# An RNN step beside an LSTM step: the RNN's product in exact bf16 parts, states of both in rings, histories copied by GpSimd

## The chip, the cores and the metric

The kernel runs on one core of one Trainium2 chip. A core has a matrix engine (TensorE, PE in the profile, its weight loads PEld), three engines for elementwise work (VectorE or DVE, ScalarE or ACT, GpSimd or POOL), a queue engine for transfers (SyncE or SP), an on-chip memory of 128 partitions (SBUF) and a smaller one that only TensorE's products land in (PSUM). The engines run side by side, each in the order of its own queue, and wait for one another through semaphores. The metric is the device time of one execution in microseconds (us); less is better.

## The reference

The program is four residual layers over x (4 sequences, 1024 steps, width 512), with a condition of 4 x 512 as the first state of both recurrences. The two recurrences matter here:

```python
xW = jnp.einsum('ntd,dh->nth', x, Wx) + b          # layer 0, RNN
def step(prev_h, xw_t):
    next_h = jnp.tanh(xw_t + prev_h @ Wh)          # 4 x 512 times 512 x 512
    return (next_h, next_h)
...
def step(carry, xw_t):                             # layer 2, LSTM
    prev_h, prev_c = carry
    A = xw_t + prev_h @ Wh                         # 4 x 512 times 512 x 2048
    i, f, o = (jax.nn.sigmoid(A[:, n * H:(n + 1) * H]) for n in range(3))
    g = jnp.tanh(A[:, 3 * H:])
    next_c = f * prev_c + i * g
    next_h = o * jnp.tanh(next_c)
    return ((next_h, next_c), next_h)
...
x = x + layer0(x); x = x + layer1(x); x = x + layer2(x); x = x + layer3(x)
```

Layer 1 is a small state-space model (SSM) with a 4-tap convolution in front; layer 3 multiplies every step by a matrix of its own for each sequence. All in fp32.

## The kernel before

All layers run in one stream. The 1024 steps lie in 32 chunks of 32 (TC). One pass of `do_pass` (L815) goes through the 32 LSTM steps of chunk c; the RNN is LEAD = 56 steps ahead of the LSTM, so the loop at L846 issues LSTM step s and RNN step s + 56 together, and around them the jobs of the layers between, each placed by hand at a step and a slot ("pe", "gap" or "end"; `do`, L841). The first 56 RNN steps run alone (the lead), the last 56 LSTM steps have no RNN. Every engine works in the order in which the loop issues its instructions; there is no planner.

The LSTM's product (`lstm_mm`, L375): h and the weights are each cut into three bf16 parts whose sum is the fp32 value exactly (`upper`, L202, takes the upper half of an fp32 word as bf16; `split`, L206, subtracts it to get the next part). The stationary operand is 12 columns, three parts of four sequences; the moving operand is one of three weight parts, 256 columns. Four products run at once in four column strips of the array. The accumulators of halves A and B (`acc2`) are turned by VectorE (L403), the three parts and the input summed by a reduction over the innermost axis (L409), gates and tanh done by ScalarE (L416, L439), products, cell and h by VectorE (L429, L434, L442), and the new h is split twice (L208). Half A's h is ready before half B's; the next step's products that need only A's half of h come first, and products of half B's gates last.

The RNN's product (`rnn_mm`, L349) is in fp32: 4 chunks of the width, 4 strips each, 4 stationary columns against 128. VectorE turns `acc0` (L368) and adds the projected input (L369); ScalarE's tanh (L372) writes the state into the history `h0`, from which the next step and the SSM read. In TensorE's queue it stands behind the LSTM's products and the step's job; in VectorE's, transpose and add stand behind the splits of half B and in front of half A's transpose of the next step.

The histories: `h0` (RNN) and `h2` (LSTM, with all three parts of each state) hold two chunks each. The SSM adds h0 to x (L461) and layer 3 adds h2 (L747). GpSimd has work only at the start.

Of the kernel before, what the change touches and what calls it, by code (L numbers as in the profile page):

```python
# [29 lines left out]
W2_BUFS = 4  # L30
NP = 3
EPS = 1e-5
XBUFS = 3


# [4 lines left out]
def cond_resid_kernel(ctx: ExitStack, tc: tile.TileContext, a: dict, out: bass.AP):  # L40
# [47 lines left out]
    def load_rows(pool, name, src, n, eng):  # L88

        t = pool.tile([P, KC, n], F32, name=name, tag=name)  # L90
        quads(eng, t, src.rearrange("(j c q) n -> j q c n", j=4, c=KC))
        return t
# [11 lines left out]
    x2 = [state.tile([P, KC, TC, B], F32, name=f"x2{i}", tag=f"x2{i}") for i in range(2)]  # L104
    xw2 = [state.tile([P, 4, KC, TC, B], F32, name=f"xw2{i}", tag=f"xw2{i}") for i in range(2)]

    h2 = [state.tile([P, KC, TC, NP, B], F32, name=f"h2{i}", tag=f"h2{i}") for i in range(2)]


    def turns(n, name, shape):  # L110
        return [state.tile(shape, F32, name=f"{name}{i}", tag=f"{name}{i}") for i in range(n)]

    tt2 = [turns(2, f"tt2{m}", [P, 4, 2, B + CT]) for m in range(2)]
    gc = [turns(4, f"gc{m}", [P, 5, 2, B]) for m in range(2)]
    prod = [turns(2, f"prod{m}", [P, 2, 2, B]) for m in range(2)]
    th2 = [turns(4, f"th2{m}", [P, 2, B]) for m in range(2)]
    tt0 = turns(1, "tt0", [P, KC, CT])
    pre0 = turns(2, "pre0", [P, KC, B])

    x1 = state.tile([P, KC, 3 + TC, B], F32, name="x1", tag="x1")  # L120
# [10 lines left out]
    quads(nc.scalar, condT, a["condT"].rearrange("(c q) j b -> j q c b", c=KC))  # L131
    load_x(0, a["xT"][0])
    wx0 = load_rows(const, "wx0", a["Wx0"], D, nc.sync)
    wh0 = load_rows(const, "wh0", a["Wh0"], D, nc.sync)

    prep_ctx = ExitStack()
    prep = prep_ctx.enter_context(tc.tile_pool(name="prep", bufs=1))
# [64 lines left out]
    def upper(x):  # L202

        return x.bitcast(BF16)[..., 1::2]

    def split(h, n):  # L206

        nc.vector.tensor_tensor(h[:, :, n], h[:, :, n - 1], upper(h[:, :, n - 1]), ALU.subtract)  # L208
# [4 lines left out]
    for h in h0:  # L213
        nc.vector.memset(h[:, :, TC - 1, :], 0.0)
    nc.vector.tensor_copy(h0[1][:, :, TC - 1, :], condT)
    nc.vector.tensor_scalar(h2[1][:, :, TC - 1, 0, :], condT, 2.0, None, ALU.mult)
    for n in range(1, NP):
        split(h2[1][:, :, TC - 1], n)
    for m in range(2):
        nc.vector.memset(gc[m][0][:, 3], 0.0)  # L220
    nc.vector.memset(x1[:, :, 0:3, :], 0.0)
# [67 lines left out]
    def split_wh2(k, g):  # L289

        w, scale, cols = layer[:, k, g], 1.0 if g == 3 else 0.5, slice(PLACE[g] * D, (PLACE[g] + 1) * D)
        part = [x[:, k, cols] for x in wh2]
        left = xw2[g % 2][:, 2 + g // 2].rearrange("p c t b -> p (c t b)")
        return (
            lambda: nc.scalar.activation(part[0], upper(w), AF.Copy, scale=scale),
            lambda: nc.vector.scalar_tensor_tensor(left, w, scale, part[0], ALU.mult, ALU.subtract),
            lambda: nc.scalar.copy(part[1], upper(left)),
            lambda: nc.vector.tensor_tensor(part[2], left, part[1], ALU.subtract),
        )
# [47 lines left out]


    def rnn_mm(c, t):  # L349
        h = h0[c % 2] if t else h0[(c - 1) % 2]  # L350
        for k in range(KC):
            for j in range(4):
                nc.tensor.matmul(  # L353
                    acc0[CT * j : CT * j + B, :],
                    h[:, k, (t - 1) % TC, :], wh0[:, k, j * P : (j + 1) * P],
                    start=(k == 0), stop=(k == KC - 1),
                )

    idle = bank("idle", [P, D], tag="ada", bufs=1)
# [1 line left out]
    def keep_busy():  # L361

        x = xin[0].rearrange("p c t b -> p (c t b)")
        tiled(idle, lambda j: x[:, :CT], x)

    def rnn_pre(c, t):
        tt, pre = tt0[0], pre0[t % 2]
        nc.vector.transpose(tt.rearrange("p c b -> p (c b)"), acc0)  # L368
        nc.vector.tensor_add(pre, xw0[c % 2][:, :, t, :], tt[:, :, :B])  # L369

    def rnn_h(c, t):
        nc.scalar.activation(h0[c % 2][:, :, t, :], pre0[t % 2], AF.Tanh)  # L372


    def lstm_mm(c, t, kh, mh, parts=range(2 * NP)):  # L375


        h = h2[c % 2] if t else h2[(c - 1) % 2]
        for x in parts:
            k, n = 2 * kh + x // NP, x % NP  # L380
            w = wh2[n][:, k].rearrange("p (g n) -> p g n", g=4)
            for j in range(4):
                n0 = P * j + 2 * CT * mh
                nc.tensor.matmul(  # L384
                    acc2[mh][CT * j : CT * j + NP * B, :],
                    upper(h[:, k, (t - 1) % TC].rearrange("p s b -> p (s b)")), w[:, :, n0 : n0 + 2 * CT],
                    start=(k == 0 and n == 0), stop=(k == KC - 1 and n == NP - 1),
                )

# [3 lines left out]
    class Half:  # L393


        def __init__(self, c, t, m):
            self.m, self.tt, self.gc, self.th = m, tt2[m][t % 2], gc[m][t % 4], th2[m][t % 4]
            self.prod, self.c = prod[m][t % 2], gc[m][(t + 1) % 4][:, 3]
            self.out = h2[c % 2][:, 2 * m : 2 * m + 2, t]


        def transpose(self, g0=0, g1=3):
# [42 lines left out]

        def split(self, n):
            split(self.out, n)

# [108 lines left out]
        nc.gpsimd.memset(r, 0.0)  # L559

    ae, xc, sq = (prep.tile([P, KC, B], F32, name=x, tag=x) for x in ("ae", "xc", "sq"))
    ones = xw2[0][:, 0, 0].rearrange("p t b -> p (t b)")
    nc.gpsimd.memset(ones, 1.0 / D)

    def mean_over_width(x):
# [115 lines left out]
    def at_step(i, f):  # L681

        c, t = divmod(i - LEAD, TC)
        at(c, t, f)
# [25 lines left out]
    for i in range(4 * KC + 3):  # L710
        for n, f in ((i - 3, 3), (i - 1, 1), (i - 2, 2), (i, 0)):
            if 0 <= n < 4 * KC:
                at_step(6 + i, stages[n][f])

    at_step(17, load_w1)
    for j in range(W2_BUFS):
        at_step((31, 33)[j // 2], lambda j=j: load_w2(j))
# [27 lines left out]

    def adapt_add(c, m, x3, t0=0, t1=TC):
        nc.vector.scalar_tensor_tensor(  # L747
            x3[:, m, :, t0:t1].rearrange("p b t -> p t b"), h2[c % 2][:, m, t0:t1, 0], 0.5, x2[c % 2][:, m, t0:t1],
            ALU.mult, ALU.add,
        )  # L750

# [63 lines left out]
    def do_pass(c, first=0, src=None, dst=None, last=None):  # L815

        lstm = c >= 0
        jobs = []
        if dst is not None:
            jobs += adapt_jobs(c - 1, dst)  # L820
        if c == NCHUNK - 1:
            more, rest = last_adapt(c, last)
            jobs += more
        if -1 <= c < NCHUNK - 1:
            jobs += ssm_jobs(c + 1)
            jobs += input_jobs(
                c + 1, 0, range(25, 29), ((28, "end"), (29, "gap"), (29, "end"), (30, "gap"))
            )
        if src is not None:
            jobs.append((9, "end", lambda: load_x(c + 4, src)))  # L830
        if c + 3 < NCHUNK:
            for m in range(KC):
                mm, end = project0(c + 3, m)
                t = (18, 20, 22, 30)[m]
                jobs += [(t, "pe", mm), (t, "end", end)]
        if lstm:
            jobs += input_jobs(c, 1, range(4), ((3, "end"), (4, "gap"), (4, "end"), (5, "gap")))
            jobs += input_jobs(c, 2, range(4, 8), ((8, "gap"), (8, "end"), (9, "gap"), (9, "end")))
            jobs += input_jobs(c, 3, range(9, 17, 2), ((15, "end"), (16, "gap"), (18, "gap"), (19, "gap")))

        def do(t, place):  # L841
            for slot, where, f in jobs:
                if (slot, where) == (t, place):
                    f()

        for t in range(first, TC):  # L846
            r = divmod(c * TC + t + LEAD, TC)
            rnn = r[0] < NCHUNK
            if lstm:
                A, Bh = Half(c, t, 0), Half(c, t, 1)  # L850
                lstm_mm(c, t, 0, 0)
                lstm_mm(c, t, 0, 1, (0, 1))
                lstm_mm(c, t, 1, 0)
                lstm_mm(c, t, 0, 1, (2, 3, 4, 5))
                lstm_mm(c, t, 1, 1)
            do(t, "pe")
            if rnn:
                rnn_mm(*r)
            if c * TC + t < 8 - TC:
                keep_busy()  # L860
            if lstm:
                A.transpose()
                A.sum()
                A.transpose_o()
                A.sum_o()
                A.gates()
                A.products()
                A.gate_o()
                Bh.transpose()
                A.cell()  # L870
                Bh.transpose_o()
                A.tanh()
                Bh.sum()
                Bh.gates()
                A.h()
                Bh.sum_o()
                A.split(1)
                Bh.gate_o()
                Bh.products()
                A.split(2)  # L880
                Bh.cell()
            do(t, "gap")
            if lstm:
                if (c, t) != (NCHUNK - 1, TC - 1):
                    for m in range(2):
                        lstm_input(c if t + 1 < TC else c + 1, (t + 1) % TC, m)
                Bh.tanh()
                Bh.h()
                Bh.split(1)
                Bh.split(2)  # L890
            if rnn:
                rnn_pre(*r)
                rnn_h(*r)
            do(t, "end")
            while later:
                later.pop()()
            for f in early.pop((c, t), ()):
                f()
        if last is not None:
            rest()  # L900
# [78 lines left out]
```

## Time and profile before

| | us |
|---|---|
| time, median of three runs | 4678.84 (4676.4 to 4680.62) |
| span of the profiled execution | 4689.2 |
| LSTM product L384, TensorE | 2908.8 busy, 98304 products |
| RNN product L353, TensorE | 1089.4 busy, 32768 records |
| transposes of the LSTM L403, VectorE | 1236.6 busy, 4096 |
| sums L409, VectorE | 1038.9 busy, 4096 |
| splits L208, VectorE | 673.2 busy, 4098 |
| RNN transpose L368 and add L369, VectorE | 316.3 and 180.2 busy, 1024 each |
| GpSimd, all | 48.7 busy, 91 instructions |

"Busy" of a group is the time in which at least one of its instructions was under way. TensorE's instructions overlap: a product is listed from its start until its result is in PSUM (273 ns for the LSTM's), while the next ones start long before. Consecutive VectorE instructions overlap too, when the later one does not need the earlier one's result.

### The profile page before, as it was taken

The page shows a single profiled execution, that of the slowest core. Times are in us where ns is not written, and L with a number is a line of the kernel's source. Part 1 is how long each engine was busy: PE and PEld are TensorE (multiplying, and loading weights), DVE is VectorE, ACT ScalarE, POOL GpSimd, SP SyncE. Part 2 cuts the span into 40 slices and gives each one's busy share as a digit, 9 for nine tenths or more (in the row PEclk, how much of TensorE's full clock was granted, in tenths as well). Part 3 has the DMA queues.
Part 4 walks back from the last instruction along what each step waited for, and adds up shares of the span by engine and source line. Part 5 has one row for each costly group of instructions (what it writes and reads, how often), then busy time and mean ns, then how long its engine had stood idle before and what let it go on. Part 6 is the DMA issues. An engine that isn't in the chain of part 4 may idle for free.

```text
span 4689.2 us, 326423 instructions
## 1 busy us (share of the span) xinstructions
PE 4552.4 (97%) x146816; PEld 3581.8 (76%) x146816; DVE 3956.1 (84%) x22102; ACT 1876.6 (40%) x9693; POOL 48.7 (1%) x91
## 2 busy tenths in 40 slices
PE   7999999999999999999999999999999999999986
PEld 5777777777877777777777877777777777777754
DVE  4688888888888888888888888888888888888876
ACT  3334444444444444443444444444443444444333
POOL 3000000000000000000000000000000000000000
PEclk9999999999999999999999999999999999999999
DMA  6300000000000000000000000000000000000000
GB/s 155 102 24 7 9 7 9 9 7 9 9 7 9 9 7 9 9 7 9 9 7 9 9 7 9 9 7 9 9 7 9 9 7 9 9 5 7 6 6 8
DMA packets 40234, 67.77 MB, mean 14 GB/s; under 512 B 8864, under 2 KB 26016, under 8 KB 38320
## 3 DMA queue, kind: packets, MB, share of 16 engines
q1 hardware_dynamic: 35792, 46.55, 3.7%
q8 instruction: 1147, 18.79, 1.7%
q14 instruction: 255, 2.09, 0.1%
q0 software_dynamic: 1696, 0.19, 0.0%
q10 hardware_dynamic: 1344, 0.14, 0.0%
HBM read 38.34 MB, written 8.39 MB: 10 GB/s over the span
## 4 chain that ended last, share of the span: by engine, by line
PE 91%; DVE 7%; issue 1%; DMA 0%; POOL 0%; ACT 0%; SPq 0%; DVEq 0%; POOLq 0%
PE acc L384 55%; PE acc L353 18%; PE proj L334 9%; PE pb L308 3%; DVE tt L403 3%; DVE gc L409 2%; PE proj L308 2%; PE ada L754 2%; DVE prod L429 1%; PE ssm_out L308 1%; DVE h L208 1%; PE idle L308 0%; PE pp L616 0%; DVE h L442 0%; DVE tt L368 0%
## 5 line engine op out<-in xcount | busy, mean ns | idle before, releaser
L384 PE MATMUL acc<-wh,h 128*12 128x256 bf16 x98304 | 2908.8, 273 | 96.6 <-DVE h L208 91.0
L384 PEld LDWEIGHTS <-h 128*12 128x12 bf16 x98304 | 2316.3, 87 | 549.0 <-DVE h L208 194.0
L403 DVE STREAM_TRANSPOSE tt<-acc 128x192 f32<-128x192 f32 (+1 forms) x4096 | 1236.6, 310 | 291.0 <-PE acc L384 267.8
L416 ACT ACTIVATE gc<-gc 128x24 f32<-128x24 f32 (+1 forms) x4096 | 854.4, 216 | 1388.5 <-DVE gc L409 1382.9
L353 PEld LDWEIGHTS acc<-wh,h 128*4 128x4 f32 x32768 | 811.6, 87 | 498.9 <-issue 204.2
L353 PE MATMUL acc<-wh,h 128*4 128x128 f32 x32768 | 1089.4, 273 | 12.4 <-ACT h L372 6.6
L409 DVE TENSOR_REDUCE gc<-tt 128x24 f32<-128x96 f32 (+1 forms) x4096 | 1038.9, 255 | 70.5
L208 DVE TENSOR_TENSOR h<-h 128x8 f32<-128x8 f32 (+1 forms) x4098 | 673.2, 164 | 69.9
L372 ACT ACTIVATE h<-pre 128x16 f32<-128x16 f32 x1024 | 221.6, 216 | 1130.9 <-DVE pre L369 1130.9
L439 ACT ACTIVATE th<-gc 128x8 f32<-128x8 f32 x2048 | 427.9, 209 | 261.9 <-DVE gc L434 225.4
L334 PE MATMUL proj<-wx,x 128*32 128x512 f32 x4096 | 530.5, 592 | 0.3 <-issue 0.3
L442 DVE SCALAR_TENSOR_TENSOR h<-gc,th 128x8 f32<-128x8 f32 x2048 | 328.8, 161 | 143.6 <-ACT th L439 133.9
L368 DVE STREAM_TRANSPOSE tt<-acc 128x128 f32<-128x128 f32 x1024 | 316.3, 309 | 68.9 <-PE acc L353 68.8
L429 DVE SCALAR_TENSOR_TENSOR prod<-gc 128x16 f32<-128x16 f32 x2048 | 348.7, 170 | 12.7
L391 ACT COPY tt<-xw 128x32 f32<-128x32 f32 x2048 | 327.9, 207 | 0.0
L434 DVE SCALAR_TENSOR_TENSOR gc<-prod 128x8 f32<-128x8 f32 x2048 | 298.6, 146 | 0.0
L369 DVE TENSOR_TENSOR pre<-xw,tt 128x16 f32<-128x16 f32 x1024 | 180.2, 176 | 37.6
L308 PE MATMUL proj<-xin,wx 128*32 128x128 f32 x4096 | 138.6, 277 | 17.5 <-DMA wh<-in_Wh_dram 11.8
L754 PE MATMUL ada<-layer,x 128*32 128x512 f32 (+1 forms) x1056 | 134.8, 587 | 2.7 <-DVE x L747 2.6
L308 PE MATMUL pb<-x,wp 128*32 128x128 f32 x4096 | 134.7, 273 | 1.0 <-issue 0.6
L308 PEld LDWEIGHTS proj<-xin,wx 128*32 128x32 f32 x4096 | 117.0, 112 | 22.1 <-DMA wh<-in_Wh_dram 11.8
L334 PEld LDWEIGHTS proj<-wx,x 128*32 128x32 f32 x4096 | 119.6, 110 | 5.5 <-issue 0.5
(125 smaller groups left out, 1159.1 us busy)
## 6 DMA issues: line engine op xcount, KB each, us to landing
layer<-in_w2T_dram SPq DMA_DIRECT2D x32, 512.0 KB, 4.6
xin<-in_xT_dram SPq DMA_DIRECT2D x128, 64.0 KB, 2.7
out_dram<-x SPq DMA_DIRECT2D x124, 64.0 KB, 2.1
wx<-in_Wx_dram SPq DMA_DIRECT2D x20, 256.0 KB, 5.1
layer<-in_Wh_dram SPq DMA_DIRECT2D x16, 256.0 KB, 6.0
wh<-in_Wh_dram SPq DMA_DIRECT2D x4, 256.0 KB, 8.3
layer<-in_w_dram SPq DMA_DIRECT2D x4, 256.0 KB, 4.5
layer<-in_base_dram SPq DMA_DIRECT2D x4, 256.0 KB, 8.1
```

What stands on the lines that cost most here:

```text
L208: nc.vector.tensor_tensor(h[:, :, n], h[:, :, n - 1], upper(h[:, :, n - 1]), ALU.subtract)
L308: nc.tensor.matmul(dst[CT * j : CT * (j + 1)], columns(j), x, start=first, stop=final)
L334: nc.tensor.matmul(ps[CT * j : CT * (j + 1), :], tok, w[:, j], start=(k == 0), stop=(k == KC - 1))
L353: nc.tensor.matmul(acc0[CT * j : CT * j + B, :], h[:, k, (t - 1) % TC, :], wh0[:, k, j * P : (j + 1) * P], start=(k == 0), stop=(k == KC - 1),
L384: nc.tensor.matmul(acc2[mh][CT * j : CT * j + NP * B, :], upper(h[:, k, (t - 1) % TC].rearrange("p s b -> p (s b)")), w[:, :, n0 : n0 + 2 ...
L391: nc.scalar.copy(tt2[m][t % 2][:, :, :, :B], xw2[c % 2][:, :, 2 * m : 2 * m + 2, t, :])
L403: nc.vector.transpose(self.tt[:, g0:g1, :, B:].rearrange("p g c b -> p (g c) b"), acc2[self.m][:, 2 * CT * g0 : 2 * CT * g1],)
L409: nc.vector.tensor_reduce(self.gc[:, to : to + g1 - g0].rearrange("p g c b -> p (g c) b"), self.tt[:, g0:g1, :, : (1 + NP) * B].rearrange( ...
L416: nc.scalar.activation(self.gc[:, g0:g1], self.gc[:, g0:g1], AF.Tanh, scale=0.5)
L429: nc.vector.scalar_tensor_tensor(self.prod, self.gc[:, 0:2], 1.0, self.gc[:, 2:4], ALU.add, ALU.mult)
L439: nc.scalar.activation(self.th, self.c, AF.Tanh, scale=0.5)
L442: nc.vector.scalar_tensor_tensor(self.out[:, :, 0], self.gc[:, 4], 1.0, self.th, ALU.add, ALU.mult)
```

## The change

From RNN step 50 on (`WHOLE`), the RNN's state and weights are cut into three bf16 parts as the LSTM's are: `rnn_mm` multiplies 12 stationary columns by each of three weight parts (`wh0p`), 12 groups of four bf16 products in place of 4 groups of four fp32 ones. The nine partial products appear as three blocks of four columns in `acc0`; `rnn_pre` sums them together with the input, which GpSimd copies beside them (`rnn_input`), by one reduction instead of an add. The state is split by two VectorE instructions of 128x16 (`rnn_split`). They are issued for the previous RNN step inside the LSTM step: the first behind half A's transpose, the second behind half A's sum; the RNN's product is issued after that (in TensorE's queue its place stays behind LSTM products and job).

The parts of both states no longer lie in the histories but in two rings of four steps each (`ring`, 96 words a step: 48 for the LSTM, 48 for the RNN). Each fourth step GpSimd copies the first parts of four steps into the histories `h2` and `h0` (`keep_h2`, `keep_h0`), and clears the other ring (`clear`). The fp32 Wh0 is loaded into a region that the LSTM's input uses later, and split in lead steps 37 to 46 (`split_wh0`); the left-overs of splitting the LSTM's weights move to `h2` and `x2`, the vector of ones to another place.

```diff
+WHOLE = LEAD - 6
+KEEP = 4
-    h2 = [state.tile([P, KC, TC, NP, B], F32, name=f"h2{i}", tag=f"h2{i}") for i in range(2)]
+    h2 = [state.tile([P, KC, TC, B], F32, name=f"h2{i}", tag=f"h2{i}") for i in range(2)]
+    ring = turns(2, "ring", [P, KEEP, KC * NP * 2 * B])
+    wide = KC * NP * B
+    def hp2(t):
+        return ring[t // KEEP % 2][:, t % KEEP, :wide].rearrange("p (c s b) -> p c s b", c=KC, s=NP)
+    def hp0(t):
+        return ring[t // KEEP % 2][:, t % KEEP, wide:].rearrange("p (c s b) -> p c s b", c=KC, s=NP)
-    tt0 = turns(1, "tt0", [P, KC, CT])
+    tt0 = turns(2, "tt0", [P, KC, B + CT])
...
+    def split_wh0(k):
+        w, left = wh0[:, k], x2[k % 2].rearrange("p c t b -> p (c t b)")
+        part = [x[:, k] for x in wh0p]
+        return (
+            lambda: nc.scalar.copy(part[0], upper(w)),
+            lambda: nc.vector.tensor_tensor(left, w, part[0], ALU.subtract),
+            lambda: nc.scalar.copy(part[1], upper(left)),
+            lambda: nc.vector.tensor_tensor(part[2], left, part[1], ALU.subtract),
+        )
...
     def rnn_mm(c, t):
-        h = h0[c % 2] if t else h0[(c - 1) % 2]
-        for k in range(KC):
+        if c * TC + t < WHOLE:
+            h = h0[c % 2] if t else h0[(c - 1) % 2]
+            parts = [(h[:, k, (t - 1) % TC, :], wh0[:, k]) for k in range(KC)]
+        else:
+            h = hp0((t - 1) % TC)
+            parts = [
+                (upper(h[:, k].rearrange("p s b -> p (s b)")), w[:, k]) for k in range(KC) for w in wh0p
+            ]
+        for n, (x, w) in enumerate(parts):
             for j in range(4):
                 nc.tensor.matmul(
-                    acc0[CT * j : CT * j + B, :],
-                    h[:, k, (t - 1) % TC, :], wh0[:, k, j * P : (j + 1) * P],
-                    start=(k == 0), stop=(k == KC - 1),
+                    acc0[CT * j : CT * j + x.shape[-1], :], x, w[:, j * P : (j + 1) * P],
+                    start=(n == 0), stop=(n == len(parts) - 1),
                 )
...
+    def rnn_input(c, t):
+        if c * TC + t >= WHOLE:
+            nc.gpsimd.tensor_copy(tt0[t % 2][:, :, :B], xw0[c % 2][:, :, t, :])
     def rnn_pre(c, t):
...
+        nc.vector.transpose(tt[:, :, B:], acc0)
+        if c * TC + t < WHOLE:
+            nc.vector.tensor_add(pre, xw0[c % 2][:, :, t, :], tt[:, :, B : 2 * B])
+        else:
+            nc.vector.tensor_reduce(
+                pre, tt[:, :, : (1 + NP) * B].rearrange("p c (s b) -> p c b s", b=B),
+                axis=mybir.AxisListType.X, op=ALU.add,
+            )
...
+    def rnn_split(c, t, n):
+        if c * TC + t >= WHOLE - 1:
+            split(hp0(t), n)
...
+    def keep_h2(c, t):
+        if t % KEEP == KEEP - 1:
+            x = kept(t)[:, :, :wide].rearrange("p t (c s b) -> p c t s b", c=KC, s=NP)
+            nc.gpsimd.tensor_copy(h2[c % 2][:, :, t - KEEP + 1 : t + 1, :], x[:, :, :, 0])
+    def keep_h0(c, t):
+        if t % KEEP == KEEP - 1 and c * TC + t >= WHOLE:
...
+            nc.gpsimd.tensor_copy(h0[c % 2][:, :, t - n + 1 : t + 1, :], x[:, :, :, 0])
+    def clear(t):
+        if t % KEEP == 1:
+            nc.gpsimd.memset(kept(t + KEEP), 0.0)
...
             do(t, "pe")
-            if rnn:
+            if rnn and not lstm:
                 rnn_mm(*r)
...
             if lstm:
                 A.transpose()
+                if rnn:
+                    rnn_split(*before, 1)
                 A.sum()
+                if rnn:
+                    rnn_split(*before, 2)
+                    rnn_mm(*r)
                 A.transpose_o()
...
                 Bh.split(2)
+                keep_h2(c, t)
             if rnn:
+                rnn_input(*r)
                 rnn_pre(*r)
                 rnn_h(*r)
+                keep_h0(*r)
+            if lstm:
+                clear(t)
```

`rnn_h` writes the tanh into the ring (`hp0`) in place of the history, and the LSTM's `h` writes into `hp2`; `lstm_mm` reads from there. In the lead's last steps, where no LSTM runs yet, the two splits stand in front of the RNN's product.

## The prediction

> **What bounds the kernel now.** I read the page first, then TensorE's order of work, then VectorE's, each over single steps in the middle of the run and over the last 56 LSTM steps, in which the RNN (which runs 56 steps ahead) is already over. The page says TensorE:
>
> ```profile
> span 4689.2 us, 326423 instructions
> PE 4552.4 (97%) x146816; PEld 3581.8 (76%) x146816; DVE 3956.1 (84%) x22102; ACT 1876.6 (40%) x9693; POOL 48.7 (1%) x91
> ...
> PE 91%; DVE 7%; issue 1%; DMA 0%; POOL 0%; ACT 0%; SPq 0%; DVEq 0%; POOLq 0%
> ...
> L353 PE MATMUL acc<-wh,h 128*4 128x128 f32 x32768 | 1089.4, 273 | 12.4 <-ACT h L372 6.6
> ```
>
> The reader is to see that a shorter RNN product (L353) seems worth its full size: TensorE is busy 97% and carries 91% of the chain of waits. The second view tests that. It is the timeline of TensorE, with columns start, length, instruction, count, and in brackets the idle time before. A step runs from one L384 (LSTM product) to the next.
>
> ```profile
> 1985.66 2.83 PE L384 MATMUL acc<-wh,h 128*12 128x256 bf16 x96
> 1988.31 1.03 PE L334 MATMUL proj<-wx,x 128*32 128x512 f32 x8
> 1989.17 1.05 PE L353 MATMUL acc<-wh,h 128*4 128x128 f32 x32
> 1990.04 2.81 PE L384 MATMUL acc<-wh,h 128*12 128x256 bf16 x96
> 1992.68 1.05 PE L353 MATMUL acc<-wh,h 128*4 128x128 f32 x32
> 1994.35 2.89 PE L384 MATMUL acc<-wh,h 128*12 128x256 bf16 x96 [0.62 <-DVE h L208]
> ```
>
> The same view near the end of the run:
>
> ```profile
> 4559.94 2.89 PE L384 MATMUL acc<-wh,h 128*12 128x256 bf16 x96 [0.63 <-DVE h L208]
> 4562.65 1.03 PE L334 MATMUL proj<-wx,x 128*32 128x512 f32 x8
> 4564.31 2.89 PE L384 MATMUL acc<-wh,h 128*12 128x256 bf16 x96 [0.63 <-DVE h L208]
> ```
>
> The first step takes 4.38 us with TensorE full: 2.65 LSTM, 0.86 of a job, 0.87 RNN. The second has no job, and TensorE idles 0.62 us, yet it takes 4.31 (with the step after it, 4.39 on average). Near the end there is no RNN at all, and a step still takes 4.37. So a loop of 4.37 to 4.39 us that does not contain the RNN sets the time; TensorE's fillers happen to fill it. The third view, VectorE in a step without extra jobs, shows this loop:
>
> ```profile
> 1911.41 0.37 DVE L208 TENSOR_TENSOR h<-h 128x8 f32<-128x8 f32 x2
> 1911.69 0.31 DVE L368 STREAM_TRANSPOSE tt<-acc 128x128 f32<-128x128 f32 x1
> 1912.04 0.18 DVE L369 TENSOR_TENSOR pre<-xw,tt 128x16 f32<-128x16 f32 x1
> 1912.71 0.38 DVE L403 STREAM_TRANSPOSE tt<-acc 128x192 f32<-128x192 f32 x1 [0.50 <-PE acc L384]
> 1913.13 0.33 DVE L409 TENSOR_REDUCE gc<-tt 128x24 f32<-128x96 f32 x1
> 1913.38 0.24 DVE L403 STREAM_TRANSPOSE tt<-acc 128x64 f32<-128x64 f32 x1
> 1913.65 0.22 DVE L409 TENSOR_REDUCE gc<-tt 128x8 f32<-128x32 f32 x1
> 1913.78 0.16 DVE L429 SCALAR_TENSOR_TENSOR prod<-gc 128x16 f32<-128x16 f32 x1
> 1913.86 0.37 DVE L403 STREAM_TRANSPOSE tt<-acc 128x192 f32<-128x192 f32 x1
> 1914.16 0.12 DVE L434 SCALAR_TENSOR_TENSOR gc<-prod 128x8 f32<-128x8 f32 x1
> ```
>
> Half B's splits end at 1911.78; TensorE then does 24 products that need them (0.65 us) and drains (0.27), and half A's transpose starts at 1912.71. From there VectorE runs without a gap into half B's transpose at 1913.86, and B's chain ends in the splits of the next step, 4.38 later. B's product itself ends at about 1913.75, so B's transpose waits for VectorE, not for TensorE. Whatever is put between A's and B's transposes lengthens the loop.
>
> **The change, part by part**, in ns a step; both ends in brackets. It acts on 968 LSTM steps; the first 40 or so are longer for other reasons (4.3 to 6.3 us), so I count 930.
>
> TensorE. LSTM: 24 groups of four products, 256 columns, in 2.65 us, 110 ns a group. RNN before: 8 such fp32 groups, 0.87 us. After: 12 bf16 groups of 128 columns; with half the columns 55 ns each, 0.66 us, or 110 if the group's pitch has another cause. I take 55, since LSTM and fp32 groups have the same pitch for the same passes times columns. It frees 0.21 us, into idle time: worth nothing but in the step of the pass with the SSM's output product (4.63 us; minus 0.16 in 32): -6 [-23 to -6; the lower end adds the 17 ns by which a mean step with RNN, 4.392, exceeds one without, 4.375].
>
> First RNN split, behind A's transpose. The row is L429 (128x16, 170 ns, the next starts 83 to 93 after it). A transpose of 192 lets an independent follower start 0.30 after it (1913.86 to 1914.16), the dependent sum only 0.42 after (1912.71 to 1913.13). The split fits there: 0 [0 to 92].
>
> Second RNN split, behind A's sum, before the transpose of o. The sum lets a follower start 0.20 (as in B) to 0.25 after it; then the split's 85 to 92. The transpose moves from 0.25 to 0.29..0.34 behind the sum: 65 [43 to 92]. Everything queued behind it moves: o's sum, the products, B's transpose, and through it the loop. ScalarE's gates end at 1913.71, before the products at 1913.78, and don't move, so they absorb nothing.
>
> On VectorE's queue, waiting costs: the first split waits for the RNN's tanh, over by 1912.47, 0.5 us early; no stall. TensorE's RNN product waits for the second split, ready about 0.8 us behind A's transpose, before the LSTM's product ends; no stall behind a job.
>
> The reduce in place of the add (L369): a sum of 32 elements holds the queue 120, one of 96 some 203 to 243, so 64 about 162, against 93; a second semaphore (GpSimd's copy) 0 to 50 more. Covered by A's transpose's wait (0.11 to 0.50 us) in 25 of 32 steps; without that cover the whole 69 to 120 counts, as in the seven steps full of SSM work: 18 [0 to 23].
>
> GpSimd. A copy of the projection each step (off the loop, two buffers), and each fourth step two 128x64 copies and a clear. The trace has GpSimd's tensor work beside VectorE only in the RNN's lead: there L369 (two SBUF inputs) took 0.18 alone and up to 0.29, 0.21 on average, under L281's 0.60 us. One h2 copy meets B's splits and one h0 copy the RNN's in four steps: 31 twice in four, 15 [0 to 55, 111 twice in four]. [...]
>
> The SSM's add of the last four RNN states (L461, 128x64) waited 0.28 for the tanh and now also for the copy, 0.4 us (between L694's 0.18 and L281's 0.60), once in 32 steps, where A's transpose follows without slack: 12 [6 to 19].
>
> Lead: six RNN steps alone in the new form, two splits longer (0.41) and 0.1 shorter on TensorE: 2 us. Splitting Wh0 (8 VectorE passes at 0.68, L296) lies under the lead's waits for TensorE (0.22 to 0.86), at most 2. The last copy of h2: under 1. The dropped strides of h2 in the residual add: nothing, it has cover.
>
> Sum: 0 + 65 + 18 + 15 + 12 - 6 = 104 ns, times 930 = 97 us, plus 3: a span of 4789. The median, 4678.8, is 10.4 below the profiled span, so 4779. Low ends: 26 ns, 24 us, 4703. High ends (TensorE at -6): 275 ns, 256 us, 4938.
>
> **Rivals.** (1) TensorE bounds, as the page's shares say: 28 of 32 steps shorten by 0.21, 0.18 x 930 = 171, 4508. Against it stand the steps without RNN at 4.37. (2) TensorE becomes the bound: groups of short products don't come faster than today's 110 ns. For: no group in the trace is faster. Place: the RNN block, 12 x 110 = 1.32, step 2.65 + 0.86 + 1.32 = 4.83 in 28 of 32, 0.44 x 0.875 x 930 = 358 over, 5050 with the rest. It decides from a pitch of about 80 ns ((4.49 - 3.51) / 12). [...] (3) VectorE takes the splits, the reduce and the copies into gaps for nothing: only TensorE's -23 remains, 930 x 0.023 = 21 less, 4658. Against it: no gap between A's and B's transposes is wide enough for the second split. (4) The splits cost their whole length, 2 x 174: 348 in place of 65, 5040. Against it: followers start 83 ns after rows of 164.
>
> **Numbers.** Forecast 0.79; (1) 0.02, (2) 0.08, (3) 0.06, (4) 0.05. Its own range is 4703 to 4938; cut at 4920 with the other cases it holds about 8 in 10, 4705 to 4920. A difference under 0.2% (9 us) can't be told from no change. Faster: (1) and most of (3), 0.06; same: the rest and the forecast's lowest edge, 0.04; slower 0.90.
>
> **What would show it.** Steps of 4.45 to 4.50 us with TensorE idle ahead of L384's successor, released by VectorE's splits; the transpose of o 0.29 to 0.34 behind A's sum; the RNN block at 0.66 us. Wrong if the RNN block takes over 0.95, if the splits under GpSimd's copies stretch by more than 0.1, or if a step stays at 4.38.

## The result, and the profile after

| | us |
|---|---|
| changed kernel, median of four runs | 4932.24 (4927.89 to 4940.77) |
| kernel before, beside it | 4677.68 (four runs) |
| ratio | 1.0545, 95% interval 1.053 to 1.056 |
| span of the profiled execution | 4929.2 (before 4689.2) |

Slower, as forecast, but by 255 us in place of 101, and 12 us above the top of the range. Between the two profiled executions the span grew by 240 us (the one of the kernel before was 10 us longer than its median). Where it went can be counted from the starts of the LSTM's products: the first of them moved from 151.4 to 172.0 us (20.6), and the mean of the 1023 steps behind it from 4.4205 to 4.6351 us (219.5).

The page of the changed kernel:

```profile
span 4929.2 us, 363974 instructions
PE 4619.2 (94%) x162400; PEld 3544.1 (72%) x162400; DVE 4160.5 (84%) x24059; ACT 1879.9 (38%) x9701; POOL 443.2 (9%) x1823
...
q8 instruction: 1274, 20.87, 1.7%
...
L388 PE MATMUL acc<-wh0p,ring 128*12 128x128 bf16 x46752 | 884.3, 219 | 32.7 <-issue 22.6
...
L509 POOL COPY h<-ring 128x64 f32<-128x64 f32 x256 | 62.2, 243 | 3273.7 <-DVE ring L496 3273.7
```

GpSimd's copies of the histories are short (243 ns) and wait for VectorE most of the time. The RNN's product (now L388) is shorter, as forecast: twelve groups take 0.63 to 0.72 us, 57 ns a group. But TensorE's counts went up, from 146816 to 162400 records of products (an fp32 product leaves two: 32768 for 16384) and as many of weight loads, and with them the line of queue q8. On the page before it was:

```profile
q8 instruction: 1147, 18.79, 1.7%
```

The columns are packets, MB and share. That TensorE's instructions come from this queue is read from the counts: 2 x 162400 records and 1361 waits are 326161 instructions, and 20.87 MB are 64 bytes for each; before, 18.79 MB stand against 293765. A packet of 16 KB then holds 256.

VectorE's timeline over one step without a disturbance (start, length, engine, line, instruction, idle time before). L457 is the LSTM's transpose, L463 its sum, L221 a split (128x16 the RNN's, 128x8 the LSTM's), L406 and L410 the RNN's transpose and reduction:

```profile
2043.06 0.37 DVE L221 TENSOR_TENSOR ring<-ring 128x8 f32<-128x8 f32 x2
2043.34 0.31 DVE L406 STREAM_TRANSPOSE tt<-acc 128x128 f32<-128x128 f32 x1
2043.75 0.27 DVE L410 TENSOR_REDUCE pre<-tt 128x16 f32<-128x64 f32 x1
2044.36 0.38 DVE L457 STREAM_TRANSPOSE tt<-acc 128x192 f32<-128x192 f32 x1 [0.34 <-PE acc L438]
2044.66 0.13 DVE L221 TENSOR_TENSOR ring<-ring 128x16 f32<-128x16 f32 x1
2044.78 0.33 DVE L463 TENSOR_REDUCE gc<-tt 128x24 f32<-128x96 f32 x1
2045.02 0.17 DVE L221 TENSOR_TENSOR ring<-ring 128x16 f32<-128x16 f32 x1
2045.10 0.25 DVE L457 STREAM_TRANSPOSE tt<-acc 128x64 f32<-128x64 f32 x1
```

The first split starts 0.30 behind A's transpose and leaves the sum at its 0.42; the second pushes the transpose of o from 0.25 to 0.32 behind the sum. The step around it takes 4.47 us. So this part went as worked out, and a clean step has the forecast's length (4.45 to 4.50).

What was not in the forecast is on TensorE. Its timeline over five steps, with L438 the LSTM's product; unbroken it takes 2.89:

```profile
2028.41 3.31 PE L438 MATMUL acc<-wh,ring 128*12 128x256 bf16 x96
...
2033.16 3.06 PE L438 MATMUL acc<-wh,ring 128*12 128x256 bf16 x96
...
2037.75 3.19 PE L438 MATMUL acc<-wh,ring 128*12 128x256 bf16 x96
...
2042.51 2.89 PE L438 MATMUL acc<-wh,ring 128*12 128x256 bf16 x96
```

The weight loads of the first of these steps show where the length comes from:

```profile
2029.38 1.52 PEld L438 LDWEIGHTS <-ring 128*12 128x12 bf16 x59 [0.21 <-DVE ring L221]
2031.33 0.10 PEld L438 LDWEIGHTS <-ring 128*12 128x12 bf16 x5 [0.43 <-issue]
```

At 2031.33, five products before the end, the stream stood still for 0.43 us with no semaphore behind it ("issue"). The DMA engines over 2026 to 2048, in 40 slices of 0.55 us, show the packets of instructions:

```profile
GB/s 0 0 0 0 0 30 0 0 0 0 0 30 0 0 0 0 0 15 45 0 0 0 0 0 30 0 0 0 0 0 0 30 0 0 0 0 0 0 30 0
...
q8 instruction: 6, 0.10, 1.8%
```

Six packets in 22 us, one every 3.3 to 3.9 us; the second lies in the slice from 2032.05 to 2032.60, about 1 us after the standstill ended. In the records this holds all along: of 462 breaks within the products, the median one ended 1.41 us behind the end of a packet (middle half 1.34 to 1.49), and the next packet started 1.16 us later (1.12 to 1.34); a packet itself took 1.07 us in the mean. One turn is 3.64 us, for 256 instructions (the shortest between two packets' starts was 3.24).

The records also show where in the stream the breaks stand. Count TensorE's products, weight loads and waits in the order of their starts: of the 309 breaks of over 150 ns with "issue" inside the LSTM's product, all 309 stand at the same place of every 256 (the 194th or 195th). In the kernel before it is 23 of 23, and in every other trace of this case all of them, at this same place. So I take a break for the stream waiting at the start of a block for its packet; the traces show the place and the times, not where a block starts. Over all passages of this place, with a break or without, 99 in 100 lie at least 1.2 us behind the end of a packet. The waits of the weight loads (us in total, times, longest) make the sum, after and then before (of the 220.4 us, 148.5 are the breaks inside the product; 71.9 stand in front of its first load, nearly all at other places of the 256):

```profile
PEld L438 <- DVE ring L221: 363.5, 1214, 1.8
...
PEld L438 <- issue: 220.4, 504, 2.2
```

```profile
PEld L384 <- DVE h L208: 194.0, 391, 1.8
...
PEld L384 <- issue: 10.9, 23, 1.2
```

From LSTM step 64 to 967, 286 of 904 steps had such a break inside the LSTM's product, 113 ns a step in the mean; before it was 16 steps and 5 ns. Steps without one had a median of 4.48 us, steps with one 4.76. (Here and in the table below a break counts with what it adds to the usual distance between two products.)

A second piece lies in the lead. VectorE's timeline near the start:

```profile
29.61 1.03 DVE L232 TENSOR_SCALAR ring<-condT 128x16 f32<-128x16 f32 x1 [21.68 <-POOL ring L230]
```

The first state is written into the ring only after GpSimd cleared it (L230), and GpSimd issues its transfers, until 28.3 us, before that. The RNN's first transpose moved from 18.9 to 33.4 us; some of it is given back while the weights are loaded.

### The profile page after: what moved, and what is told of

It reads as the page before. It is cut to its first block, busy times and chain, and to the rows that moved or that the text cites. A ratio compares the mean times of both kernels' runs of the same rounds, so it can differ in the third digit from the quotient of the medians.

```text
span 4929.2 us, 363974 instructions
## 1 busy us (share of the span) xinstructions
PE 4619.2 (94%) x162400; PEld 3544.1 (72%) x162400; DVE 4160.5 (84%) x24059; ACT 1879.9 (38%) x9701; POOL 443.2 (9%) x1823
## 3 DMA queue, kind: packets, MB, share of 16 engines
q8 instruction: 1274, 20.87, 1.7%
## 5 line engine op out<-in xcount | busy, mean ns | idle before, releaser
L438 PE MATMUL acc<-wh,ring 128*12 128x256 bf16 x98304 | 3007.7, 273 | 224.9 <-DVE ring L221 80.0
L438 PEld LDWEIGHTS <-ring 128*12 128x12 bf16 x98304 | 2277.8, 87 | 846.5 <-DVE ring L221 363.5
L457 DVE STREAM_TRANSPOSE tt<-acc 128x192 f32<-128x192 f32 (+1 forms) x4096 | 1238.3, 310 | 267.5 <-PE acc L438 251.6
L388 PEld LDWEIGHTS <-ring 128*12 128x12 bf16 x46752 | 781.6, 88 | 421.6 <-issue 249.9
L463 DVE TENSOR_REDUCE gc<-tt 128x24 f32<-128x96 f32 (+1 forms) x4096 | 1041.3, 256 | 36.9
L221 DVE TENSOR_TENSOR ring<-ring 128x8 f32<-128x8 f32 (+1 forms) x6046 | 967.0, 160 | 70.8 <-ACT ring L420 0.6
L388 PE MATMUL acc<-wh0p,ring 128*12 128x128 bf16 x46752 | 884.3, 219 | 32.7 <-issue 22.6
L420 ACT ACTIVATE ring<-pre 128x16 f32<-128x16 f32 x974 | 210.5, 216 | 1228.9 <-DVE pre L410 1228.9
L496 DVE SCALAR_TENSOR_TENSOR ring<-gc,th 128x8 f32<-128x8 f32 x2048 | 329.3, 161 | 144.0 <-ACT th L493 133.9
L406 DVE STREAM_TRANSPOSE tt<-acc 128x128 f32<-128x128 f32 x1024 | 316.3, 309 | 53.0 <-PE acc L388 52.9
L509 POOL COPY h<-ring 128x64 f32<-128x64 f32 x256 | 62.2, 243 | 3273.7 <-DVE ring L496 3273.7
L410 DVE TENSOR_REDUCE pre<-tt 128x16 f32<-128x64 f32 x974 | 258.8, 266 | 102.5 <-DVE tt L406 2.3
L402 POOL COPY tt<-xw 128x16 f32<-128x16 f32 x974 | 189.5, 209 | 254.1 <-DVE pre L410 254.1
L519 POOL MEMSET ring<- 128x384 f32 x256 | 106.9, 417 | 599.5 <-DVE gc L488 297.4
L830 PE MATMUL ada<-layer,x 128*32 128x512 f32 (+1 forms) x1056 | 141.1, 587 | 2.8 <-DVE x L823 2.7
```

The source lines that it names most:

```text
L388: nc.tensor.matmul(acc0[CT * j : CT * j + x.shape[-1], :], x, w[:, j * P : (j + 1) * P], start=(n == 0), stop=(n == len(parts) - 1),)
L406: nc.vector.transpose(tt[:, :, B:], acc0)
L438: nc.tensor.matmul(acc2[mh][CT * j : CT * j + NP * B, :], upper(h[:, k].rearrange("p s b -> p (s b)")), w[:, :, n0 : n0 + 2 * CT], start=( ...
L457: nc.vector.transpose(self.tt[:, g0:g1, :, B:].rearrange("p g c b -> p (g c) b"), acc2[self.m][:, 2 * CT * g0 : 2 * CT * g1],)
L463: nc.vector.tensor_reduce(self.gc[:, to : to + g1 - g0].rearrange("p g c b -> p (g c) b"), self.tt[:, g0:g1, :, : (1 + NP) * B].rearrange( ...
L496: nc.vector.scalar_tensor_tensor(self.out[:, :, 0], self.gc[:, 4], 1.0, self.th, ALU.add, ALU.mult)
```

## The experiments

Theory S (supply): TensorE's instructions come in blocks of 256, and a block takes about 3.64 us; the loss depends on how many instructions a step has. Theory V: VectorE's chain and what collides with it is longer than counted. Per step a kernel's instructions are its total over 1024; "breaks" is the mean of the standstills inside the LSTM's product, steps 64 to 967, from the trace's records. "Supply" is 1.16 + packet + 1.41 us, times instructions a step, over 256. e11 is e3's edit with e2's, e12 is e1's with e4's; e5 and e9 are the changed kernel as it is.

| run | instr. a step | packet us | supply us a step | breaks ns | step us | time us | ratio |
|---|---|---|---|---|---|---|---|
| before | 287 | 1.118 | 4.13 | 5 | 4.400 | 4678 | 1 |
| after | 319 | 1.067 | 4.53 | 113 | 4.624 | 4932 | 1.0545 |
| e1 fp32 product | 287 | 1.105 | 4.12 | 3 | 4.499 | 4798 | 1.0238 |
| e2 no splits | 318 | 1.111 | 4.57 | 171 | 4.639 | 4937 | 1.0542 |
| e3 one weight part | 258 | 1.100 | 3.70 | 1 | 4.498 | 4789 | 1.0218 |
| e4 clear on VectorE | 319 | 1.128 | 4.61 | 203 | 4.724 | 5012 | 1.0701 |
| e5 control | 319 | 1.107 | 4.58 | 181 | 4.696 | 4998 | 1.0674 |
| e6 two weight parts | 288 | 1.112 | 4.14 | 8 | 4.504 | 4809 | 1.0273 |
| e7 fp32 in halves | 348 | 1.100 | 4.99 | 414 | 5.053 | 5341 | 1.1409 |
| e9 control | 319 | 1.064 | 4.53 | 126 | 4.637 | 4932 | 1.0543 |
| e10 no splits | 318 | 1.060 | 4.51 | 96 | 4.528 | 4830 | 1.0331 |
| e11 one part, no splits | 257 | 1.061 | 3.65 | 0 | 4.408 | 4698 | 1.0046 |
| e12 fp32, clear on VectorE | 287 | 1.063 | 4.12 | 0 | 4.496 | 4780 | 1.0223 |

The kernel before stood at 4687, 4682 and 4676 us beside e1 to e4, e5 to e8 and e9 to e12, which ran on three chips, one for each group of four. 95% intervals are about 0.0015 to either side (0.0013 for e11).

**The RNN's product: e1, e3, e6.** e1 multiplies the ring's first part in fp32 and doesn't split Wh0:

```diff
-            parts = [
-                (upper(h[:, k].rearrange("p s b -> p (s b)")), w[:, k]) for k in range(KC) for w in wh0p
-            ]
+            parts = [(h[:, k, 0], wh0[:, k]) for k in range(KC)]
...
```

> The changed kernel with the RNN's product back in fp32 (16 instructions a step in place of 96, TensorE 0.87 us in place of 0.66), read from the first part in the ring; splits, reduction, rings and GpSimd copies stay, the second and third part are computed and not read; Wh0 is not split. Theory S (supply): the 96 short instructions of the product bring TensorE to a standstill inside the LSTM product that follows (in the changed kernel's trace 294 of 904 steps, 116 ns a step on average), and that is what my sum lacked. It expects those standstills to go and the time to come near my forecast: 4790 to 4830, although TensorE has more to do. Theory V (VectorE): the splits, the reduction and the copies cost more than I summed, and TensorE's standstills lie in time that VectorE takes anyway. It expects 4915 to 4935, no change.

Counted as everywhere else here, weight loads and both records of an fp32 product included, it is 64 instructions a step, not 16. e3 keeps one of Wh0's parts, e6 two (`[:2]`):

```diff
-... for k in range(KC) for w in wh0p
+... for k in range(KC) for w in wh0p[:1]
```

> The changed kernel with one weight part in place of three in the RNN's product: 32 instructions a step, TensorE about 0.22 us (this leaves out the products with the two lower weight parts). VectorE and GpSimd unchanged. Theory S expects no standstills and 4790 to 4830, the same as with the fp32 product although TensorE has 0.65 us less to do. Theory V expects 4915 to 4935. If it comes out clearly under the fp32 product's time, TensorE's length still counts.

> Leaves out the products with the third part of Wh0. Theory S (TensorE's instructions come in blocks of 256, and a block takes about 1.16 us from the end of one standstill to the next packet, 1.07 us for the packet and 1.41 us from its end to the next instruction, 3.64 us in all): the step has 192 + 64 + some 30 instructions, 286, which can be had in 4.07 us, under the clean step's 4.48: no standstills, 4785 to 4810, as with one part. Rival R (the standstills belong to the short bf16 products themselves, so many ns each): two thirds of the products leave about half the loss between one part (4789) and three (4932): 4850 to 4890.

Measured: e1 4798.20, ratio 1.0238 (1.0223 to 1.0253); e3 4788.84, 1.0218 (1.0201 to 1.0235); e6 4809.41, 1.0273 (1.0258 to 1.0289). The whole of VectorE's and GpSimd's part of the change is still in these kernels, so V falls. One and two parts and fp32 differ by 0.5% at most, though the product keeps TensorE busy for 0.40 us with one part and 1.05 in fp32; from two parts to three, on one chip (e6 and e5), it jumps by 4.0%, 189 us. That is no price for each product (rival R of e6) but a threshold: 288 instructions a step are had in 4.14 us, less than the 4.50 that VectorE's chain takes, and 319, at 4.58, are not. The supply column gives the threshold and not the step: with three parts and the splits the mean step is 0.09 to 0.12 us over the column. How breaks and VectorE's chain add up within a step was not worked out. The weight loads' waits in e3, and the second of them in e6:

```profile
PEld L438 <- DVE ring L221: 762.8, 1513, 1.8
...
PEld L438 <- issue: 36.9, 54, 2.0
```

```profile
PEld L438 <- issue: 141.1, 264, 2.0
```

The row alone would mislead for e6. Inside the product, at the one place of 256, stand 5.6 us of e3's 36.9 and 20.3 of e6's 141.1, against 148.5 of the changed kernel's 220.4; the rest is in front of the product's first load. So the breaks nearly go, and TensorE waits for VectorE's splits instead: in this kernel the chain of VectorE is the bound again.

**More instructions, no bf16 in the RNN: e7**, on top of e1's edit.

```diff
+        halves = (0,) if c * TC + t < WHOLE else (0, 64)
+        for q in halves:
+            for n, (x, w) in enumerate(parts):
+                for j in range(4):
+                    n0, n1 = q, q + P // len(halves)
+                    nc.tensor.matmul(
+                        acc0[CT * j : CT * j + x.shape[-1], n0:n1], x, w[:, j * P + n0 : j * P + n1],
...
```

> The fp32 product of e1 cut into two halves of 64 columns: the same columns streamed and no bf16 product, but 128 instructions in place of 64. Theory S: 350 instructions at 3.64 us for 256 take 4.98 us, over the step's 4.50: the step goes to 4.98 to 5.15 and the time to 5240 to 5400. Rival R (short bf16 products): no standstills, 4795 to 4830.

Measured 5341.37, ratio 1.1409 (1.1392 to 1.1427). TensorE's timeline (L437 LSTM, L387 RNN, L360 a job):

```profile
2032.34 1.06 PE L387 MATMUL acc<-wh,ring 128*4 128x64 f32 x64
2033.24 2.67 PE L437 MATMUL acc<-wh,ring 128*12 128x256 bf16 x88
2036.35 0.39 PE L437 MATMUL acc<-wh,ring 128*12 128x256 bf16 x8 [0.44 <-issue]
...
2038.34 0.83 PE L437 MATMUL acc<-wh,ring 128*12 128x256 bf16 x24
2040.10 2.14 PE L437 MATMUL acc<-wh,ring 128*12 128x256 bf16 x72 [0.93 <-issue]
```

The RNN's block keeps its 0.9 us (2032.34 to 2033.24), as with whole products, and yet the step goes from 4.50 to 5.05: the LSTM's product, which was not touched, is broken up. The supply column says 4.99. All but 15 of the 717 waits in this row stand at the one place of 256:

```profile
PEld L437 <- issue: 496.4, 717, 2.0
```

This run shows S without any bf16 product in the RNN.

**The splits: e2, e10, e11.**

```diff
     def rnn_split(c, t, n):
-        if c * TC + t >= WHOLE - 1:
-            split(hp0(t), n)
+        pass
```

> The changed kernel without the two VectorE splits of the RNN's state: the second and third parts stay zero (this leaves out the lower 16 bits of the state in the RNN's product). Theory S expects the standstills to stay and only the second split's place on VectorE to be won back, 65 to 80 ns in 930 steps: 4855 to 4875. Theory V expects most of the loss to go: 4700 to 4760.

Measured 4937.46, ratio 1.0542 (1.0525 to 1.0559): no gain at all beside the changed kernel's 1.0545, which neither theory had expected, and which would have read as "the splits cost nothing". But the changed kernel had not run on that chip. With its control, and in a kernel without breaks:

> The changed kernel once more, as the control for the next one: its time went from 4932 to 4998 between two chips, with a mean 16 KB instruction packet of 1.067 and 1.107 us. By theory S each further ns of the mean packet is worth about 1.2 us (1274 packets one after another): 4930 to 5015, to be read from its own packets: 4932 + 1.2 to 1.7 times the ns over 1067.

> e2 again, without the RNN's splits (the second and third parts of h0 are left at zero), this time with a control on its chip. Its clean steps were 85 ns shorter than the changed kernel's (medians 4397 and 4482). If the supply of TensorE's instructions alone sets the time, the control's time less 0 to 10. If the supply's standstills lie on top of VectorE's chain in part of the steps, 20 to 75 less.

> One weight part and no splits, in a kernel that has no standstills: leaves out the products with the other two parts of Wh0 and the second and third parts of h0. Against one part with splits (ratio 1.0218), this gives the price of the two splits on VectorE's chain. The prediction's 65 ns a step: 60 us less, ratio 1.009, 4722 to 4735. The 85 ns that the clean steps showed: 4705 to 4720. Nothing: 4780 to 4795. The splits' whole length of 334 ns: under 4500, which TensorE's 4.2 to 4.3 us would not allow.

e9 4931.81, ratio 1.0543 (1.0527 to 1.0559); e10 4829.79, 1.0331 (1.0317 to 1.0345); e11 4698.21, 1.0046 (1.0033 to 1.0058). Beside its control, leaving the splits out saves 102 us, more than the 20 to 75 expected: the clean steps' median falls from 4.476 to 4.388 (88 ns), and the breaks fall too (126 to 96 ns a step). In the kernel without breaks the difference e3 less e11 is 0.0172, 80 us, 86 ns a step (two chips, so by their ratios; the mean steps differ by 85 to 90). e11's 4698 lies below even the 4705 to 4720 expected of 85 ns; the kernel before was 10 us faster on its chip than on e3's. e11's page and TensorE's timeline:

```profile
PE 4101.2 (87%) x131232; PEld 3035.8 (65%) x131232; DVE 4019.9 (86%) x22111; ACT 1877.4 (40%) x9701; POOL 439.8 (9%) x1823
```

```profile
2034.03 0.40 PE L388 MATMUL acc<-wh0p,ring 128*12 128x128 bf16 x16
2034.84 2.89 PE L437 MATMUL acc<-wh,ring 128*12 128x256 bf16 x96 [0.41 <-DVE ring L221]
2037.56 1.03 PE L362 MATMUL proj<-wx,x 128*32 128x512 f32 x8
2038.41 0.40 PE L388 MATMUL acc<-wh0p,ring 128*12 128x128 bf16 x16
2039.23 1.04 PE L437 MATMUL acc<-wh,ring 128*12 128x256 bf16 x31 [0.42 <-DVE ring L221]
```

The RNN's product here is 0.4 us in place of 0.9, TensorE is busy 87% in place of the kernel before's 97%, and the step is 4.38 to 4.39 all the same, with 0.41 us of TensorE idle in front of the LSTM's product: the loop that does not contain the RNN, as the prediction read it.

**The first clearing: e4, e5, e12.**

```diff
     for x in ring:
-        nc.gpsimd.memset(x, 0.0)
+        nc.vector.memset(x, 0.0)
```

> The changed kernel with the rings' first clear done by VectorE in place of GpSimd, where it stands behind the transfers that GpSimd issues. In the changed kernel's trace VectorE waits 21.68 us for it, and RNN step 0 is turned at 33.4 us against 18.9 before; by step 40 the gap is 11 to 15. Both theories: 11 to 15 us less, 4917 to 4921. If the later waits of the lead (for weights) take it up, less than 3.

> The changed kernel itself, beside the others of this call, as a control for e4. If the 80 us by which the kernel with VectorE's clearing was longer belong to that program, this one gives 4925 to 4942 again. If they belong to the chip or the hour of that call, it gives 4990 to 5020.

> e1 (fp32 product, no standstills) with the first clearing of the rings on VectorE in place of GpSimd. If the clearing's place behind GpSimd's transfers costs the time before the first LSTM step and nothing gives it back, the first LSTM product starts some 8 to 15 us earlier than e1's 161.5 and the ratio goes from 1.0238 to 1.0205 to 1.0222. If it's hidden behind the loads of the LSTM's weights, 1.023 to 1.0245.

e4 gave 5012.17, ratio 1.0701 (1.0685 to 1.0717), 80 us more than the changed kernel where 11 to 15 less were expected. e5, the changed kernel itself on yet another chip, gave 4998.26, 1.0674 (1.0656 to 1.0692), while the kernel before moved by 0.2% only. So most of those 80 us are not the clearing's, and e4's trace shows where they are: its first LSTM product starts at 155.1 us, 10 to 17 before that of the changed kernel, and its mean step behind that is 4.73 us in place of 4.64. (The changed kernel as it is did not run on e4's chip.) The table has what goes with them: the packet took 1.067 and 1.064 us where the kernel gave 4932, 1.107 where it gave 4998, 1.128 in e4. From e9 to e5, 66 us for 42 ns, 1.6 us a ns; 1274 packets one after another would make 1.27. e1 and e12, with 287 instructions a step, had packets of 1.105 and 1.063 and differ by no more than their intervals. Whether the clearing itself is worth anything is then only to be seen in e12 against e1: the first LSTM product starts at 154.3 in place of 161.5 us, and the ratio is 1.0223 (1.0209 to 1.0237) against 1.0238 (1.0223 to 1.0253). 7 us by the trace; the intervals overlap, so by the times it stays open.

**A version of the kernel before: e8.** Half B's sum issued ahead of its second transpose:

```diff
-                Bh.transpose_o()
                 A.tanh()
                 Bh.sum()
+                Bh.transpose_o()
```

> Not the change but the kernel before with half B's sum issued ahead of its second transpose on VectorE, as a version that may beat both. If VectorE's chain sets the step, B's sum starts about 0.1 us earlier and TensorE's 4.38 us become the bound: 4655 to 4672. If TensorE sets it already, or what is put off is late in its turn, 4680 to 4695.

Measured 4720.20, ratio 1.0082 (1.0067 to 1.0097): slower, a miss. The last steps, which have no RNN, take 4.414 in place of 4.375 us, so the loop without the RNN grew, presumably by what was put off; this was not followed further. No version that beats both kernels came out of the runs.

## Why the prediction was wrong in size

**The term that failed** is TensorE's: "It frees 0.21 us, into idle time: worth nothing but in the step of the pass with the SSM's output product ... -6 [-23 to -6]". The length was right (57 ns a group where 55 was taken). Its ground, passes times columns, no run shows as such: the records show columns (110 ns for a group of 256 in bf16 and for one of 128 in fp32, 57 for 128 in bf16) and no passes. But the product was costed by its length alone. It has 96 instructions a step where the fp32 one has 64 (the page before shows this: 32768 records for 16384 products, each with its weight load), and the stream of instructions had little to spare (287 of them a step at 4.13 us, in a step of 4.40). In its place the runs show 1.0545 - 1.0218 = 0.0327 of 4680, 153 us, between three parts and one (two chips; on one chip, three parts against two, 189 us). Of the 126 ns by which the mean step of the changed kernel exceeds e3's, 113 are breaks inside the LSTM's product. Without this term the forecast's sum comes close: the two kernels that keep the rest of the change and have almost no breaks, e3 and e1, lie 102 and 111 us over the kernel before, and the working had 97 + 3. Part of that is luck: by the traces 85 to 92 us lie in the steps and 10 to 14 ahead of the first LSTM product, so the steps came out under the 97 and the lead over the 3.

The other steps, in their order:

- **What bounds the kernel:** right. e11 shortens the RNN's product to less than half and stays at the old step.
- **The two splits**, 0 + 65, and 15 for collisions with GpSimd: 86 ns a step in e11 against e3 and 88 in the clean steps of e10 against e9, in sum 6 to 8 over. The parts are not as put: the second split moved the transpose of o by 0.07 as worked out, and the LSTM's splits (128x8) that lie under GpSimd's copies of `h2` took 166 to 170 ns and followed each other at 0.20 us, as those without a copy. So the contention term was 0 on these instructions. That leaves about 20 more than 65 for the splits' own place; which of the two it belongs to was not found.
- **Reduction, 18, and the SSM's add, 12:** for the second semaphore the prediction put 0 to 50 ns, an estimate without a row; the reduction starts 0.41 us behind the RNN's transpose (median, L406 to L410) where the add stood at 0.34, and what made these 0.07 is not shown. What is left of e11 over the kernel before is 0.0046, 21 us, with the lead in it, and its mean step is 8 ns longer. The step with the add (the ninth of a pass) is 508 ns longer in e11 (4.907 against 4.399), 16 ns as a mean over 32. That leaves nothing for the reduction's 18, but e11's TensorE product is much shorter than the forecast's, and its gain (up to 23 in the prediction) could hide some of it: the two can't be told apart here.
- **The lead, 3 us:** 13 to 21 us for the changed kernel (first LSTM product at 164.7 to 172.0 in its three traces, before 151.4). Missed: the clearing behind GpSimd's transfers, 21.7 us of waiting at the start, partly given back. It is the second error, and a small one.
- **Rivals.** (1) and (3) fall by the sign. (2) named TensorE as the bound, and in a third of the steps it was, but by another mechanism: the RNN's 48 products take 14 ns each, 57 a group, where it put 110. (4), whole length, 348: the runs say 86.
- **Signs to look for.** The RNN block at 0.66, the transpose of o at 0.32, clean steps at 4.48: all there, and the time was still wrong by 153 us. The signs asked about each term of the sum and none about the time that a mean step takes beyond a clean one.

The runs show packets of 16 KB, 256 instructions of 64 bytes, and breaks at one place of every 256. Of the changed kernel's 1274 packets no two overlap: each starts 3.24 us or more behind the one before and takes 1.07 in the mean.

What stays open: how many packets' instructions TensorE has at hand at a time, which no run shows; why a packet takes 1.06 us in e9 to e12 and 1.10 to 1.13 in e1 to e8 (other chips, but also other hours; the two can't be told apart here); whether the 1.41 and 1.16 us of a turn can be shortened; and why the time follows the packet's length somewhat more than one for one. That the next packet is asked for when the stream enters a new block is inferred: at a break it starts 1.16 us behind the one place of 256. In e11, without breaks, it starts 0.36 us behind it in the median, so the request would then come some time before the block's first instruction runs; this was not tried.

## What to carry to other kernels

Cost a matrix product by its instructions as well as by its columns: count TensorE's records, weight loads included, over a step, and compare 256 of them with the turn of the instruction queue (here 3.6 us, to be read from the breaks without a releaser and the packets of the "instruction" queue). The sign that tells such a break from other waits without a releaser is its place: always the same one of every 256 instructions. In these runs the breaks came to 8 ns a step or less where the step's instructions were had in 4.14 us or less, and to 96 to 414 ns where they took 4.51 and more; there the breaks fall on whatever stands in the stream, here above all on the LSTM's product, which the change didn't touch. And where a kernel sits on such a limit, compare only with a control on the same chip (the changed kernel gave 4932 on one and 4998 us on another).

## What the runs showed that was not expected

- When the stream ran short, 256 TensorE instructions took about 3.6 us, with 1.06 to 1.13 us for the packet of 16 KB and 2.6 us around it, while the queue's packets took 1.7% of the sixteen DMA engines' time. All 309 breaks inside the LSTM's product stand at one place of every 256 instructions.
- The same program took 4932 us in two measurements and 4998 in a third, on another chip than the second, while the kernel before, with 10% fewer TensorE instructions, stayed within 0.3% (4676 to 4687).
- 48 bf16 products of 128 columns in four strips take 0.68 us without a break, 14 ns each.
- VectorE's splits (128x8) with both operands in SBUF kept their 0.17 us under GpSimd copies of 0.24 us.
